# Turning the 8 x 20 cells of each sampling slot so that the eight ky lie side by side

## The chip, the core and the metric

The kernel runs on one core of a Trainium2 chip. Its time is the device time of one execution in microseconds (us). The five engines are named as the profile names them: PE (matrix unit, with PEld for its weight loads), DVE (vector unit), ACT (activation unit), POOL (general unit) and SP, which here only issues DMAs.

## The reference, cut to what matters

There are 32 images of 128 channels and 32 x 32 pixels. Two layers run in turn, each on group-normalised input and each added to its input.

The first layer is a state-space convolution along the 1024 pixels (1024 inner channels), a gated linear unit, a layer norm and a decoder. The second layer, which the change touches, is a deformable convolution with an 8 x 8 kernel:

```python
off = depthwise_3x3(x) + offset_b               # per pixel: 64 x offsets, 64 y offsets
px, py = gx + kx + off_x, gy + ky + off_y       # for each of the 64 taps (ky, kx)
s = bilinear_sample(x, py * 32/31 - 0.5, px * 32/31 - 0.5)
acc += s * weight[channel, tap]                 # then batch norm, exact gelu, + x
```

A bilinear sample is a sum over input pixels, weighted with hat functions: `hat(d) = max(0, 1 - |d|)` of the distance in x, times the hat of the distance in y.

## The kernel before, in words

**First layer, first half (0 to about 1302 us).** The state-space convolution runs on PE and leaves `y_d` in DRAM. The change does not touch it.

**Main block (about 1302 us to the end).** Two streams are interleaved for each image by `run_along`, which orders the code by planned costs while the program is being built, so that each engine's order is fixed: `first_part(b + 2)` (gated unit, norm, decoder: the matmuls of lines L808, L831, L847, L736) and `second_part(b)` (the deformable convolution of an image two behind). The schedule is manual: each engine works through its instructions in the order in which the code issues them.

**The deformable part.** All 64 taps of all pixels are re-indexed by `u = x + kx` (39 values) and `v = y + ky`. For one u, the up to eight kx that reach it are its *slots*. The 17 entries of `PACKS` group the u's into packs of up to 16 slots; the slots of an image sum to 256. Inside a slot lie `CELLS = 8 * NV = 160` cells: eight ky, each with 20 values of v, in the order "k v" (v is the fast index). Partitions 0 to 63 hold the low side of the v range and 64 to 127 the high side; in each half the 64 partitions are an 8 x 8 window of input pixels.

The steps for one pack, with the names that the profile shows:

1. `prepare` (for the next image) makes the offsets `dco`, then `drel` (L940, L948, L957, L968 on DVE), lays them out in DRAM as `rel_d`, gathers them into the tile `dr` (L999) and, for each of the eight window columns k, makes x hats on ACT: `dh` = relu(1 - |dr - k|) (L1010, L1011), stored to DRAM as `dhat`.
2. `load_x` fetches the x hats of a pack into the S tile `ds` (L1110), with SP issuing; `load_y` fetches `dhy`, the y distances, straight from `rel_d` (L1125), broadcast to the partitions of a side.
3. `hat_y` on ACT turns `dhy` into y hats in place (L1145, L1146).
4. `weights` on DVE multiplies `ds` by `dhy`, in place, in four parts of a quarter of the slots (L1151): the hat product. When two parts are done it calls `load_y` for a later pack, because the `dhy` buffer is free then (three buffers).
5. The matmuls of L1227 take the S tile as the moving operand and a window of pixels `dxw` as weights (64 rows, 128 columns), and write to PSUM tiles `dps` (four buffers). A pack has four *pieces*, each for both sides. Piece 0 holds the image's edge, in five small blocks; pieces 1 to 3 have all eight ky and four v each, cut into two windows of two v. The two sides use different rows of the array and start in pairs. Each fp32 matmul is two records in the trace (two passes).
6. `scale` on DVE multiplies `dps` by the tap weights into `prod` (L1243), in `(slot, ky, v)` order.
7. POOL adds the eight ky rows of `prod` (L1269) and then the slots into `dacc` (L1275).

**Order around the change.** For pack h, `second_part` issues on PE the matmuls of pieces 0 and 1; then DVE's `scale` calls for them, with `hat_y(h + 1)` on ACT beside them; then DVE's four `weights(h + 1)`; then PE's matmuls of pieces 2 and 3, and their `scale` calls; then `load_x(h + 2)` and POOL's sums. The four PSUM buffers hold exactly two pieces of two sides, so each half pack of matmuls waits until DVE has scaled the half before it. Matmuls of `first_part` stand between the halves. The steps of `prepare` hang on a list of due times: `due` counts 12 places per pack, and for example the nine `taps` are due at places 44 to 68.

The read and the write of the matmuls are these, for a slot count m:

```python
to = [t[:, lo:hi].rearrange("p (s k v) -> p s k v", s=m, k=rows) for t in ps]
ap = [frm.ap[0], [CELLS, m], [step * NV + skew, rows], [1, r1 - r0]]
nc.tensor.matmul(to[side][:, :, :, r0:r1], xw[half, w, :], frm, start=True, stop=True)
```

Of the kernel before, what the change touches and what calls it, by code (L numbers as in the profile page):

```python
# [9 lines left out]
AF = mybir.ActivationFunctionType  # L10
# [5 lines left out]
P = 128  # L16
# [499 lines left out]
NV = 20  # L516
VBASE = (1, 18)
# [15 lines left out]
)  # L533
NWIN = 7
BOUND_X, BOUND_Y = 2.45, 2.45
HSUB = NCOL // P


def span_of(u):
# [50 lines left out]
def main_block(nc, tc, const, ins, x, u_d, y_d, x1_d, out, offmax):  # L590
# [21 lines left out]
    with ctx:  # L612
# [271 lines left out]
        def prepare(b):  # L884
# [112 lines left out]
            def gather():  # L997
                t = st["t"] = one.tile([P, HSUB], F32, tag="rel", name=f"dr_{b}")
                nc.sync.dma_start(  # L999
                    t, at(rel_d[b % 2], 0, [[HSUB, P // 2], [SIDE, 2], [1, HSUB]])  # L1000
                )

            def hat(k):


                def run():
                    if k == 0:
                        st["h"] = dram.tile([2, 8, SIDE], F32, tag="hat_d", name=f"dhat_{b}")
                    t = hatpool.tile([P, HSUB], F32, tag="hat", name=f"dh_{b}_{k}")
                    nc.scalar.activation(t, st["t"], AF.Abs, bias=minus[:, k : k + 1])  # L1010
                    nc.scalar.activation(t, t, AF.Relu, scale=-1.0, bias=const["one"])  # L1011
                    nc.scalar.dma_start(
                        at(
                            st["h"], k * SIDE,
                            [[HSUB, P // 2], [8 * SIDE, 2], [1, HSUB]],
                        ),
                        t,
                    )

                return run  # L1020
# [127 lines left out]
        def weights(h, part):  # L1148

            cut, t = cut_of(h, part)  # L1150
            nc.vector.tensor_mul(s_of[h][:, cut], s_of[h][:, cut], t)  # L1151
            if part % 2:
                q = 2 * h + part // 2
                hy_of.pop(q)
                load_y(q + HB)
# [15 lines left out]
        def second_part(b, steps):  # L1171


            steps = sorted([*steps, *ending], key=lambda e: e[0])
            ending.clear()
            acc = one.tile([P, W, H], F32, tag="acc", name=f"dacc_{b}")
            nc.gpsimd.memset(acc, 0.0)
            for n in range(NP):
                x0, us = PACKS[n]
                m = slots_of(n)  # L1180
                xw = xw_of[b, x0]
                windows(b, n + 1)
                prod = prods[(b * NP + n) % 2]

                h = b * NP + n
                s = s_of.pop(h)

                for i in range(0, PIECES, 2):

                    def due(j):  # L1190
                        while steps and steps[0][0] <= 3 * (PIECES * n + i) + j:
                            steps.pop(0)[1]()

                    due(0)
                    work = []
                    if i > 0 and h + 1 < len(packs):
                        for part in range(PARTS):
                            weights(h + 1, part)
                    for piece in (i, i + 1):
                        ps = [  # L1200
                            psam.tile(
                                [P, 512], F32, tag="sam", name=f"dps_{b}_{n}_{piece}_{side}"
                            )
                            for side in range(2)
                        ]
                        lo = 0
                        for parts in zip(blocks_of(0, piece), blocks_of(1, piece)):
                            rows, run = parts[0][0][1], parts[0][0][3]
                            hi = lo + rows * run * m
                            to = [  # L1210
                                t[:, lo:hi].rearrange("p (s k v) -> p s k v", s=m, k=rows)
                                for t in ps
                            ]
                            for part in range(len(parts[0][1])):
                                for side in range(2):
                                    (ky, _, v0, _, step, skew), wins = parts[side]
                                    w, r0, r1 = wins[part]
                                    half = slice(64 * side, 64 * side + 64)
                                    frm = s[half, 0, ky * NV + v0 - VBASE[side] + r0 :]
                                    frm = bass.AP(  # L1220
                                        tensor=frm.tensor, offset=frm.offset,
                                        ap=[
                                            frm.ap[0], [CELLS, m],
                                            [step * NV + skew, rows], [1, r1 - r0],
                                        ],
                                    )
                                    nc.tensor.matmul(  # L1227
                                        to[side][:, :, :, r0:r1],
                                        xw[half, w, :], frm, start=True, stop=True,
                                    )  # L1230
                            for side in range(2):
                                work.append((piece, side, to[side], parts[side][0]))
                            lo = hi
                    yield measure(m)

                    def scale(piece, side):
                        for p, sd, frm, (ky, rows, v0, run, step, skew) in work:
                            if (p, sd) != (piece, side):
                                continue
                            wt = wk[:, table_of[n] : table_of[n] + m]  # L1240
                            wt = wt[:, :, ky : ky + step * (rows - 1) + 1 : step]
                            at_y = prod[:, ky * KS + v0 - ky :]
                            nc.vector.tensor_mul(  # L1243
                                bass.AP(
                                    tensor=at_y.tensor, offset=at_y.offset,
                                    ap=[
                                        at_y.ap[0], [H, m],
                                        [step * (KS - 1) + skew, rows], [1, run],
                                    ],
                                ),  # L1250
                                frm,
                                wt[:, :, :, None].to_broadcast([P, m, rows, run]),
                            )

                    for j in range(4):
                        due(1 + j)
                        scale(i + j // 2, j % 2)
                        if i == 0 and h + 1 < len(packs):
                            hat_y(h + 1, j)
                        yield measure(m)  # L1260
                    due(5)
                    yield measure(m)
                load_x(h + SB)

                def row(ky):
                    return prod[:, ky * KS : ky * KS + m * H]

                for to, frm in ((2, 0), (3, 1), (4, 6), (5, 7), (2, 4), (3, 5), (2, 3)):
                    nc.gpsimd.tensor_add(row(to), row(to), row(frm))  # L1269
                total = row(2)  # L1270
                slot = 0
                for u in us:
                    j0, nj = span_of(u)
                    to = acc[:, u - 7 + j0 : u - 7 + j0 + nj]
                    nc.gpsimd.tensor_add(  # L1275
                        to, to,
                        total[:, slot * H : (slot + nj) * H].rearrange(
                            "p (s y) -> p s y", y=H
                        ),
                    )  # L1280
                    slot += nj

            o = two.tile([P, L], F32, tag="img", name=f"do_{b}")
            xr = two.tile([P, L], F32, tag="img", name=f"dxr_{b}")
            nc.sync.dma_start(xr, x1_d[b])
            nc.gpsimd.tensor_scalar(  # L1286
                o.rearrange("p (h w) -> p w h", w=W), acc, bn_mean, bn_inv,
                op0=ALU.subtract, op1=ALU.mult,
            )
            ending.append((6, lambda: nc.scalar.activation(o, o, AF.Gelu, bias=bn_beta)))  # L1290
            ending.append((11, lambda: nc.vector.tensor_add(o, o, xr)))
            ending.append((14, lambda: nc.scalar.dma_start(out[b], o)))
# [183 lines left out]
```

## Time and profile before

| | |
|---|---|
| median of 3 runs | 12768.52 us (12756.01 to 12776.53) |
| the profiled execution | 12769.27 us, its span 12767.5 us |
| mean granted PE clock | 0.972 |
| busy over the span | PE 96%, DVE 65%, POOL 63%, ACT 43% |
| main block (1302 to 12768 us) | 11466 us; busy PE 11025.0, DVE 7544.7, POOL 7489.9, ACT 4942.4 us |
| packs in the main block | 32 x 17 = 544, so 21.1 us each |

How to read it. A row of the groups of instructions names the line, the engine, the operation, the tiles (out<-in) with shapes and the number of instructions; after the bar come busy us in total, mean ns of one, and how long the engine had idled just before, with what ended that idling. The list of waits has us in total, times, and the longest. PE counts as busy whenever a matmul is in flight, so 96% does not mean that it runs at its best rate: a slow matmul is busy too.

### The profile page before, as it was taken

How to read it: one execution, taken by the hardware profiler on the slowest of the kernel's cores; microseconds unless marked ns; L12 is line 12 of the kernel's file. 1: busy time of each engine (PE TensorE's matmuls, PEld its weight loads, DVE VectorE, ACT ScalarE, POOL GpSimd, SP SyncE). 2: the span in 40 equal slices, each digit the busy share in tenths (PEclk: the TensorE clock that was granted, in tenths of full speed). 3: DMA queues.
4: the chain of work that ended last, by engine and by line, in shares of the span. 5: the costliest groups of instructions: out<-in, count | busy, mean ns of one | idle time of the engine just before them, and what ended most of it. 6: DMA issues, size and time to landing. Idle time of an engine off the chain costs nothing.

```text
span 12767.5 us, 157327 instructions
## 1 busy us (share of the span) xinstructions
PE 12216.4 (96%) x51362; PEld 6679.5 (52%) x51362; DVE 8277.2 (65%) x14315; ACT 5490.5 (43%) x7823; POOL 8094.1 (63%) x6987
## 2 busy tenths in 40 slices
PE   7999999999999999999999999999999999999965
PEld 7999444444444444444444444444444444444444
DVE  5555126666666667666666666666666666666667
ACT  4344124444444444444444444444444444444443
POOL 2555126666666676666666666667666666666668
PEclk9999999999999999999999999999999999999976
DMA  7899136666666666667666776666666667667666
GB/s 238 268 278 276 68 90 177 181 181 186 180 183 181 179 176 183 182 175 184 183 181 177 186 187 180 178 176 173 183 181 176 184 176 186 180 183 187 179 183 180
DMA packets 1521915, 2350.16 MB, mean 184 GB/s; under 512 B 619586, under 2 KB 835266, under 8 KB 1520066
## 3 DMA queue, kind: packets, MB, share of 16 engines
q1 hardware_dynamic: 1382210, 2027.97, 60.4%
q10 hardware_dynamic: 89728, 177.76, 3.8%
q0 software_dynamic: 49152, 134.28, 3.5%
q8 instruction: 413, 6.77, 0.2%
q14 instruction: 412, 3.38, 0.1%
HBM read 2016.61 MB, written 407.02 MB: 190 GB/s over the span
## 4 chain that ended last, share of the span: by engine, by line
PE 78%; DMA 7%; DVE 5%; POOL 3%; issue 2%; ACT 2%; SPq 2%; ACTq 0%; DVEq 0%; POOLq 0%
PE gpv L831 24%; PE gpg L808 23%; PE dps L1227 16%; PE psy L320 5%; PE psz L237 3%; DMA ds<-dhat 3%; PE gpo L736 3%; PE gph L847 3%; DVE ds L1151 2%; DVE prod L1243 2%; POOL prod L1269 1%; DMA dhy<-rel_d 1%; SPq L1125 1%; POOL do L1286 1%; DMA dxw<-dxw_d 1%
## 5 line engine op out<-in xcount | busy, mean ns | idle before, releaser
L1269 POOL TENSOR_TENSOR prod<-prod 128x512 f32<-128x512 f32 (+3 forms) x3808 | 4994.8, 1343 | 1614.0 <-DVE prod L1243 1571.4
L1243 DVE TENSOR_TENSOR prod<-dps,k_weight_slots 128x512 f32<-128x512 f32 (+16 forms) x8704 | 3126.1, 408 | 1437.5 <-PE dps L1227 1128.2
L808 PE MATMUL gpg<-gy,g_w_glu 128*128 128x512 f32 x8192 | 3771.8, 603 | 41.0 <-ACT gs L815 27.0
L831 PE MATMUL gpv<-gy,g_w_glu 128*128 128x512 f32 x8192 | 3751.7, 600 | 0.0
L1151 DVE TENSOR_TENSOR ds<-ds,dhy 128x640 f32<-128x640 f32 (+2 forms) x2176 | 2821.2, 1342 | 620.7 <-DMA ds<-dhat 354.8
L1227 PE MATMUL dps<-ds,dxw 64*128 64x128 f32 (+14 forms) x23936 | 2778.3, 375 | 364.4 <-DVE prod L1243 329.5
L1227 PEld LDWEIGHTS dps<-ds,dxw 64*128 64x128 f32 x23936 | 1979.9, 197 | 1455.5 <-DVE prod L1243 560.5
L808 PEld LDWEIGHTS gpg<-gy,g_w_glu 128*128 128x128 f32 x8192 | 1522.7, 191 | 1965.0 <-issue 1910.6
L831 PEld LDWEIGHTS gpv<-gy,g_w_glu 128*128 128x128 f32 x8192 | 1514.0, 190 | 1887.3 <-issue 1887.3
L869 POOL TENSOR_TENSOR gs<-gs,gq 128x512 f32<-128x512 f32 x448 | 647.2, 1445 | 2257.2 <-ACT gq L868 2257.2
L1145 ACT ACTIVATE dhy<-dhy,k_minus_y 128x640 f32<-128x640 f32 (+2 forms) x2176 | 1699.1, 781 | 532.5 <-DMA dhy<-rel_d 197.7
L1146 ACT ACTIVATE dhy<-dhy,one 128x640 f32<-128x640 f32 (+2 forms) x2176 | 1726.5, 793 | 71.1
L868 ACT ACTIVATE gq<-gr 128x512 f32<-128x512 f32 x448 | 281.4, 628 | 2556.9 <-DVE gr L860 2555.6
L839 DVE SCALAR_TENSOR_TENSOR gs<-gpv,k_b_glu,gs 128x512 f32<-128x512 f32 x512 | 384.2, 750 | 1374.8 <-PE gpv L831 1296.9
L815 ACT ACTIVATE gs<-gpg,k_b_glu 128x512 f32<-128x512 f32 x512 | 351.6, 687 | 1867.3 <-PE gpg L808 1722.0
L1275 POOL TENSOR_TENSOR dacc<-dacc,prod 128x256 f32<-128x256 f32 (+6 forms) x1184 | 1048.1, 885 | 92.8
L357 POOL DMA_DIRECT2D y_d<-yo x1024 | 590.0, 583 | 690.6 <-ACT yo L344 641.2
L320 PE MATMUL psy<-toe,z 128*128 128x192 f32 x4096 | 668.0, 326 | 7.4 <-DVE z L242 5.5
L320 PEld LDWEIGHTS psy<-toe,z 128*128 128x128 f32 x4096 | 663.3, 196 | 11.4 <-DVE z L242 6.8
L738 POOL TENSOR_TENSOR gs<-gs,gr 128x512 f32<-128x512 f32 x448 | 652.3, 1456 | 0.0
L335 DVE TENSOR_TENSOR psy<-psy,t 128x256 f32<-128x256 f32 (+2 forms) x768 | 333.8, 435 | 345.9 <-ACT t L328 329.1
L847 PE MATMUL gph<-gu,k_W_enc 128*128 128x512 f32 x1024 | 522.9, 592 | 0.0
(164 smaller groups left out, 6046.8 us busy)
## 6 DMA issues: line engine op xcount, KB each, us to landing
dhy<-rel_d SPq DMA_DIRECT2D x3264, 160.0 KB
ds<-dhat SPq DMA_DIRECT2D x832, 400.0 KB
ds<-dhat SPq DMA_DIRECT2D x448, 480.0 KB
dxw<-dxw_d SPq DMA_DIRECT2D x832, 224.0 KB
y_d<-yo POOLq DMA_DIRECT2D x1024, 128.0 KB, 4.1
gy<-y_d SPq DMA_DIRECT2D x512, 256.0 KB
u<-u_d SPq DMA_DIRECT2D x224, 512.0 KB
dhat<-dh ACTq DMA_DIRECT2D x256, 390.0 KB
```

The costliest lines, as they stand in the source:

```text
L320: nc.tensor.matmul(ps[:, c // 2, c % 2, :], rows[i][:, (g * CG + c0 + c) // 2, c % 2, :], toe[:, c0 + c, :], start=True, stop=True,)
L738: nc.gpsimd.tensor_add(sums[0], sums[0], r)
L808: nc.tensor.matmul(gate, w_glu[:, k, D + m * P : D + m * P + P], ys[k], start=(k == 0), stop=(k == KD - 1),)
L831: nc.tensor.matmul(val, w_glu[:, k, m * P : m * P + P], ys[k], start=(k == 0), stop=(k == KD - 1),)
L847: nc.tensor.matmul(h, w_enc[:, m * P : (m + 1) * P], u, start=True, stop=True)
L1145: nc.scalar.activation(t, t, AF.Abs, bias=minus_y)
L1146: nc.scalar.activation(t, t, AF.Relu, scale=-1.0, bias=const["one"])
L1151: nc.vector.tensor_mul(s_of[h][:, cut], s_of[h][:, cut], t)
L1227: nc.tensor.matmul(to[side][:, :, :, r0:r1], xw[half, w, :], frm, start=True, stop=True,)
L1243: nc.vector.tensor_mul(bass.AP(tensor=at_y.tensor, offset=at_y.offset, ap=[at_y.ap[0], [H, m], [step * (KS - 1) + skew, rows], [1, run],], ...
L1269: nc.gpsimd.tensor_add(row(to), row(to), row(frm))
L1275: nc.gpsimd.tensor_add(to, to, total[:, slot * H : (slot + nj) * H].rearrange("p (s y) -> p s y", y=H),)
```

## The change

It turns the order of cells inside a slot from "k v" to "v k": for each v the eight ky lie side by side.

- **x hats.** `gather` and `hat` use 104 partitions with 960 elements (six whole slots) each instead of 128 with 780, so that the turn can be made inside a partition. The first ACT pass of `hat` reads `dr` in (s, v, k) order, thus with a step of 20 elements, and writes contiguously. The store to `dhat` has 104 rows of 960 elements.
- **y hats.** `dhy` stays in "k v" order. The hat product (L1151) walks `ds` contiguously and reads `dhy` with a step of 20 elements.
- **Matmuls.** They read `ds` with ky as the fast index and write PSUM in (s, v, k) order. For pieces 1 to 3 a read and a write are runs of 2 x 8 = 16 contiguous elements, where they were runs of 2. For the two-row blocks of piece 0 the read becomes runs of 2 where it was 6, 4 or 2; the four-row block reads runs of 4 where it read single elements.
- **Scale.** DVE reads `dps` turned back, `"p s v k -> p s k v"`, so its PSUM source has a step of 8 elements in pieces 1 to 3 and of 2 in the two-row blocks. `prod` is written as before.

The number and the order of matmuls, DVE, ACT and POOL instructions and of the DMAs stay as they are, but for the two fills of `rel_n` at the start, which move by a place or two. Because a matmul now writes another pattern of a PSUM buffer than the one before it there, the program gains some 1090 waits in PE's queue, two ahead of each pack's matmuls of pieces 2 and 3: for PE's own counter, at a value that the matmuls of pieces 0 and 1 reach. The diff, without its context lines:

```diff
-HSUB = NCOL // P
+ROWS = 104
+HSUB = NCOL // ROWS
...
-                    t, at(rel_d[b % 2], 0, [[HSUB, P // 2], [SIDE, 2], [1, HSUB]])
+                    t[:ROWS], at(rel_d[b % 2], 0, [[HSUB, ROWS // 2], [SIDE, 2], [1, HSUB]])
...
-                    nc.scalar.activation(t, st["t"], AF.Abs, bias=minus[:, k : k + 1])
-                    nc.scalar.activation(t, t, AF.Relu, scale=-1.0, bias=const["one"])
+                    t = t[:ROWS]
+                    nc.scalar.activation(
+                        t.rearrange("p (s v k) -> p s v k", v=NV, k=8),
+                        st["t"][:ROWS].rearrange("p (s k v) -> p s v k", v=NV, k=8),
+                        AF.Abs, bias=minus[:ROWS, k : k + 1],
+                    )
+                    nc.scalar.activation(t, t, AF.Relu, scale=-1.0, bias=const["one"][:ROWS])
...
-                            [[HSUB, P // 2], [8 * SIDE, 2], [1, HSUB]],
+                            [[HSUB, ROWS // 2], [8 * SIDE, 2], [1, HSUB]],
...
-            nc.vector.tensor_mul(s_of[h][:, cut], s_of[h][:, cut], t)
+            x = s_of[h][:, cut].rearrange("p s (v k) -> p s v k", k=8)
+            nc.vector.tensor_mul(x, x, t.rearrange("p s (k v) -> p s v k", k=8))
...
-                                t[:, lo:hi].rearrange("p (s k v) -> p s k v", s=m, k=rows)
+                                t[:, lo:hi].rearrange("p (s v k) -> p s v k", s=m, k=rows)
...
-                                    frm = s[half, 0, ky * NV + v0 - VBASE[side] + r0 :]
+                                    frm = s[half, 0, (v0 - VBASE[side] + r0) * 8 + ky :]
...
-                                            [step * NV + skew, rows], [1, r1 - r0],
+                                            [8, r1 - r0], [step + 8 * skew, rows],
...
-                                        to[side][:, :, :, r0:r1],
+                                        to[side][:, :, r0:r1, :],
...
-                                frm,
+                                frm.rearrange("p s v k -> p s k v"),
```

## The prediction

> **What bounds the kernel now.** I read the page's busy table, then its groups of instructions for the four lines that the change alters, then the waits, and last a timeline of one ordinary pack. PE is the engine to follow, and the changed matmuls (L1227) have 15.9% of the chain that ended last. From the page:
>
> ```profile
> PE 12216.4 (96%) x51362; PEld 6679.5 (52%) x51362; DVE 8277.2 (65%) x14315; ACT 5490.5 (43%) x7823; POOL 8094.1 (63%) x6987
> ```
>
> From the groups by shape, the widest L1227 group, and the rows that price a strided access on DVE:
>
> ```profile
> L1227 PE MATMUL dps<-ds,dxw 64*128 64x256 f32 x9216 | 1533.4, 452 | 37.7 <-DVE prod L1243 34.1 <-ACT gn_r L914 2.9 <-ACT dvt L1032 0.7
> ...
> L1151 DVE TENSOR_TENSOR ds<-ds,dhy 128x640 f32<-128x640 f32 x1728 | 2286.1, 1362 | 562.0 <-DMA ds<-dhat 341.4 <-ACT dhy L1146 170.5 <-DMA dxw<-dxw_d 19.4
> L1243 DVE TENSOR_TENSOR prod<-dps,k_weight_slots 128x512 f32<-128x512 f32 x2304 | 1582.4, 687 | 145.9 <-PE dps L1227 21.4 <-DVE prod L1243 2.7
> ...
> L839 DVE SCALAR_TENSOR_TENSOR gs<-gpv,k_b_glu,gs 128x512 f32<-128x512 f32 x512 | 384.2, 750 | 1374.8 <-PE gpv L831 1296.9 <-ACT dhy L1146 60.3 <-ACT gs L815 17.6
> ...
> L957 DVE SCALAR_TENSOR_TENSOR drel<-dco,k_base_x 128x1024 f32<-128x1024 f32 x32 | 64.2, 2005 | 0.0
> ```
>
> From the waits: matmuls that wait for a PSUM buffer which DVE has yet to scale, and the hat product waiting for its operands:
>
> ```profile
> PEld dps L1227 <- DVE prod L1243: 560.5, 359, 18.8
> DVE ds L1151 <- DMA ds<-dhat: 354.8, 196, 13.8
> PE dps L1227 <- DVE prod L1243: 329.5, 124, 18.5
> ...
> DVE ds L1151 <- ACT dhy L1146: 209.5, 106, 33.4
> ```
>
> So PE mostly runs on, and when it stops it stops for DVE. How near DVE is shows in the second half of an ordinary pack (timelines of PE and of DVE):
>
> ```profile
> 6127.79 2.40 PE L1227 MATMUL dps<-ds,dxw 64*128 64x256 f32 x16
> ...
> 6138.05 2.29 PE L1227 MATMUL dps<-ds,dxw 64*128 64x192 f32 x26
> ```
>
> ```profile
> 6125.80 6.29 DVE L1151 TENSOR_TENSOR ds<-ds,dhy 128x640 f32<-128x640 f32 x4
> 6132.00 3.07 DVE L1243 TENSOR_TENSOR prod<-dps,k_weight_slots 128x512 f32<-128x512 f32 x4
> ```
>
> The last scale ends at 6135.07, the next pack's matmuls start at 6138.05: **3.0 us of slack** in a pack of 21.1 us. In the packs that also carry `prepare` there is none: L918, L936, L940, L948, L957 and L968 have 591 us of DVE, 18.5 us per image, due at places 42 to 74, that is in about 3 of 17 packs (12 places each).
>
> [...] successive pairs of passes start 267 ns apart at 256 columns in runs of 2 (1.04 ns per column), 112 ns at 128 columns in runs of 4 (0.88), 140 ns at 64 single columns (2.19). [...] The trace has a stepped destination (L957, 32 words): by L839's 750 ns at 512 and 1.04 ns per column, 1024 columns should take 1283 ns; they take 2005, which is 0.71 more per column. No DVE row of before has a stepped source. [...] L1151 runs from 477 to 1947 ns (all shapes), POOL's L1269 averages 1412.
>
> **The change part by part.** Slots sum to 256 x 32 = 8192.
>
> *Matmuls, pieces 1 to 3.* A pack has 3 pieces x 2 windows x 2 passes = 12 paired passes of 16 columns per slot: 8192 x 192 = 1.573 million columns. From 1.04 to 0.85 ns (runs of 16; between the 0.83 of an L808 record, 512 columns every 428 ns, and the 0.88 above): **-300 us**.
>
> *Matmuls, piece 0.* The 6- and 4-wide blocks go from long runs to runs of 2: 8192 x (24 + 16) columns x about 0.17 = +56. The four-row block goes from single elements to runs of 4: from 2.19 to no less than the 106 ns of a weight load (1.66 per column), 8192 x 8 x 0.5 = -33. Net **+25 to +30**.
>
> *New waits in PE's queue.* Two per pack for PE's own counter: the matmuls that they wait for ended a half pack earlier, so only issuing them can cost. The semaphore instructions at L1227 have a median of 51 ns: 0 to 1,090 x 0.051 = +56 us. Most stands beside the running matmul, as such waits do in piece 3 already (pairs still 267 ns apart); I take **+20**. PE alone is then worth **-250 us** where it is the bound, which it is but for the waits.
>
> *Hat product, L1151.* Columns: 1728 x 640 + 320 x 480 + 128 x 320 = 1.300 million. I take 0.70 (L957 0.71[...]): **+910 us of DVE, +1.7 us per pack** (910 / 544). [...] I see no gain here. POOL[...] is held longer too; it has 65% of the main block, and DVE waited on it for 117.8 us only. Queued behind L1151 on DVE stand the scale of pieces 2 and 3, L839 and L860; PE waits for the scale, ACT's L868 for L860. `load_y` leaves later as well, but one and a half packs ahead of its use.
>
> *Scale, L1243.* Pieces 1 to 3: 8192 x 192 = 1.573 million columns with a step of 8; piece 0: 8192 x 48 = 0.393 million with a step of 2. Price of a stepped PSUM source: unknown, from 0 to the 0.70 of SBUF, so 0 to **+1,376 us** (2.5 us per pack). I take 0 as a little likelier: nothing in the trace says that PSUM has SBUF's limit. Below 0 there is no room, since 687 ns for 512 is already one column per 1.04 ns and a fixed part.
>
> *x hats on ACT.* 256 times two passes from 780 to 960 elements at 0.83 ns (L906 at 1024: 1148, L1011 at 780: 946): +77 us; the stepped read of L1010 adds 0 to 172 (0.70 x 960 x 256). ACT is at 43% and the hats are due at 109 to 172, `ready` at 178, thus hidden by at least half a pack; without that cover a hat delays `load_x` of the next image by under 2 us, 32 times. Cost 0 (0 to +60). *DMAs*: the same bytes in 104 rows for 128, and no added issue on SP, ACT or POOL: 0 (-10 to +10). *Fill of `rel_n`*: still two pieces per tile, once: 0.
>
> *Sum for the likeliest case.* DVE's +1.7 us per pack fits the 3.0 us of an ordinary pack. It does not fit the 3 packs with `prepare`: 3 x 32 x 1.7 = 163 us. Nor fully where the product starts late already: 302 times, 564 us, 1.9 us each, leaving 1.1; they lose 0.6 x 302 = 181. New waits 344, PE gain 250: **+94 us**. The profiled execution (12769.27, span 12767.5) lies 1 us off the median, so this counts from 12768.5: **12,860 us**. Its own range is 12,700 (late packs lose nothing) to 13,000.
>
> **Rivals.**
>
> *Faster: the new DVE work stays in its slack.* If the stepped `dhy` costs under 0.35 per column and PSUM nothing, +0.85 us or less per pack fits even the 1.1 us of late packs; only the `prepare` packs lose (0 to 80 us). Then 12,768 - 250 + 40 = **12,560** (12,500 to 12,740). For it: DVE is at 66% of the main block. [...] It decides below 1.1 us per pack.
>
> *Much slower: PSUM reads pay as well.* 1.7 + 2.5 = 4.2 us per pack exceeds the 3.0: every pack loses 1.2, 544 x 1.2 = 653, minus 250: **13,170** (13,000 to 13,350). DVE would be at (7,545 + 910 + 1,376) / 11,850 = 83%, and PE would wait for it in every pack. For it: the singles on SBUF pay on PE and DVE alike. Against: PSUM is another memory.
>
> *The matmuls don't quicken.* If 1.04 comes from two row tiles running together and not from the runs, the gain is gone and 12,768 + 344 + 20 = 13,130. Against it: the runs of 4 also run in pairs, at 0.88.
>
> **How the numbers follow.** Faster rival 0.36, likeliest case 0.36, PSUM rival 0.24, no quickening 0.04. A change within 0.2% (26 us) is what a measurement of this kernel can't tell from none. The likeliest case spreads over both sides of that: faster 0.04, within 0.08, slower 0.24. Sum: faster 0.40, same 0.08, slower 0.52. I leave out the lowest and highest ends: 12,520 to 13,230. The likeliest case is the forecast.
>
> **What would show it.** Right: 64x256 passes with a mean well under 452 ns; L1151 at 640 columns near 1.8 us; L1243 at 512 still near 690; the waits of L1227 for L1243 up by some 300 us. L1243 near 1,045 means the PSUM rival, L1151 below 1.6 us the faster one. The forecast is wrong if L1227's waits stay at 560.5 and 329.5, or if L1227 does not quicken.

## The result, and the profile after

The changed kernel takes **12,935.3 us** (median of 4 runs, 12,930.8 to 12,954.7) against 12,768.8 us beside it: ratio **1.0136, 95% interval [1.0124, 1.0148]**, 167 us slower. The forecast was 12,860. Its profiled execution took 12,954.7 us (span 12,951.6, granted clock 0.955).

The page's busy table of the changed kernel:

```profile
PE 12125.7 (94%) x51362; PEld 6754.3 (52%) x51362; DVE 8917.0 (69%) x14315; ACT 5785.3 (45%) x7823; POOL 8977.8 (69%) x6987
```

PE is busy 91 us less in a span that is 184 us longer. DVE gained 640 us of busy time, and POOL 884, though the change gives POOL nothing new. The groups by shape of the changed kernel (L1234, L1158 and L1250 were L1227, L1151 and L1243; after the bar: busy us, mean ns of one):

```profile
L1158 DVE TENSOR_TENSOR ds<-ds,dhy 128x640 f32<-128x640 f32 x1728 | 2799.1, 1664 | 565.8 <-DMA ds<-dhat 335.9 <-ACT dhy L1152 180.7 <-DMA dxw<-dxw_d 18.8
L1250 DVE TENSOR_TENSOR prod<-dps,k_weight_slots 128x512 f32<-128x512 f32 x2304 | 1584.7, 688 | 127.4 <-PE dps L1234 2.9 <-DVE prod L1250 2.7
...
L1234 PE MATMUL dps<-ds,dxw 64*128 64x256 f32 x9216 | 1382.2, 413 | 74.8 <-DVE prod L1250 69.5 <-ACT gn_r L915 2.9 <-ACT dvt L1038 0.7
```

The wide matmuls went from 452 to 413 ns (successive pairs start 216 ns apart instead of 267, 0.84 ns per column), the hat product from 1362 to 1664 ns, the scale with its stepped PSUM read from 687 to 688. POOL's sums beside them, before and in the changed kernel (groups):

```profile
L1269 POOL TENSOR_TENSOR prod<-prod 128x512 f32<-128x512 f32 (+3 forms) x3808 | 4994.8, 1343 | 1614.0 <-DVE prod L1243 1571.4
```

```profile
L1276 POOL TENSOR_TENSOR prod<-prod 128x512 f32<-128x512 f32 (+3 forms) x3808 | 5492.4, 1472 | 1440.6 <-DVE prod L1250 1397.8
```

The waits of PE and of its weight loads in the changed kernel (us in total, times, longest):

```profile
PE dps L1234 <- DVE prod L1250: 451.0, 168, 17.1
PE dps L1234 <- DMA dhy<-rel_d: 91.1, 12, 9.4
PE gpm L759 <- POOL gs L739: 64.4, 30, 2.6
```

```profile
PEld dps L1234 <- DVE prod L1250: 714.1, 346, 17.4
```

The waits for the scale (`prod`) rose from 329.5 and 560.5. PE's wait for POOL was 2.1 us before: now the layer norm's matmul (L759) stands waiting for it about once per image.

Averages hide the place, so I read the trace pack by pack: from the first matmul of a pack to that of the next, averaged over 28 of the 32 images, in us. Kernels named here are those of the experiments below.

```
pack           1      2      5      6      8      9   other 11   all 17   PE idle
before       17.30  21.41  20.59  22.58  16.80  22.95   222.1     343.8      9.1
changed      20.12  22.14  21.02  25.89  18.75  23.30   217.1     348.3     16.5
y in order   17.46  21.13  20.02  21.86  17.82  23.38   216.8     338.4     11.7
10 stepped   17.43  21.13  20.02  21.88  17.64  23.29   217.0     338.4     11.9
pairs        17.50  21.15  20.00  23.03  17.93  23.29   216.0     339.0     12.0
pairs+fill   17.51  21.15  20.00  22.66  18.59  21.19   216.4     337.5      9.0
```

Eleven packs are 5 us per image faster in the changed kernel. Packs 1, 6 and 8 lose 8.1 us, packs 2, 5 and 9 another 1.5. Besides, the first matmul of L1234 starts at 1874.9 us, L1227's at 1853.0: 22 us are lost once, ahead of the first pack.

Pack 6 of one image shows how. PE's timeline before (start, us, and in brackets how long PE had been idle and for whom):

```profile
5424.28 2.01 PE L1227 MATMUL dps<-ds,dxw 64*128 64x192 f32 x22
5426.99 1.32 PE L1227 MATMUL dps<-ds,dxw 64*128 64x256 f32 x6 [0.70 <-DVE prod L1243]
5428.24 3.70 PE L831 MATMUL gpv<-gy,g_w_glu 128*128 128x512 f32 x8
```

and in the changed kernel:

```profile
5494.58 2.49 PE L1234 MATMUL dps<-ds,dxw 64*128 64x192 f32 x20 [1.75 <-DVE prod L1250]
5497.73 2.07 PE L1234 MATMUL dps<-ds,dxw 64*128 64x256 f32 x6 [0.66 <-DVE prod L1250]
5499.73 4.78 PE L832 MATMUL gpv<-gy,g_w_glu 128*128 128x512 f32 x8
```

The hat product ahead of this pack's first scale is what came later (DVE's timelines, before and changed):

```profile
5413.46 6.23 DVE L1151 TENSOR_TENSOR ds<-ds,dhy 128x640 f32<-128x640 f32 x4
```

```profile
5482.45 8.05 DVE L1158 TENSOR_TENSOR ds<-ds,dhy 128x640 f32<-128x640 f32 x4
```

PE's wait grew by 1.7 us. But the pack also lost time while PE worked: eight passes of `gpv` that the change doesn't touch took 4.78 us instead of 3.70. The window of this pack (its length in us, then busy us of PE, PEld, DVE, ACT and POOL, then the granted clock, the DMA share and GB/s) says why; before:

```profile
5424.28:5446.42 22.14, 21.44 (x82) 10.36 (x81) 17.65 (x26) 7.17 (x12) 18.46 (x14) 1.00 0.60 155
```

and in the changed kernel:

```profile
5492.24:5518.58 26.34, 23.93 (x81) 12.04 (x80) 19.44 (x29) 7.17 (x12) 22.14 (x15) 0.87 0.63 154
```

The granted clock fell from 1.00 to 0.87. The trace's clock records know only full and half; in all they hold 726 us at half clock before and 1,159 us after.

Pack 1 loses time by another way: there PE waits for POOL. Its window in the same image, before and in the changed kernel:

```profile
5321.02:5338.43 17.41, 17.41 (x76) 8.78 (x75) 16.25 (x27) 12.97 (x16) 14.50 (x13) 1.00 0.40 127
```

```profile
5385.81:5404.93 19.12, 17.05 (x75) 8.63 (x75) 15.95 (x26) 13.05 (x16) 18.67 (x14) 1.00 0.41 119
```

POOL, busy 14.50 of 17.41 us before, is now busy 18.67 of 19.12 us, and PE stands 2.1 us for it.

### The profile page after: what moved, and what is told of

Same layout as the page of the kernel before. It is cut to its first block, busy times and chain, and to the rows that moved or that the text cites. A ratio compares the mean times of both kernels' runs of the same rounds, so it can differ in the third digit from the quotient of the medians.

```text
span 12951.6 us, 158419 instructions
## 1 busy us (share of the span) xinstructions
PE 12125.7 (94%) x51362; PEld 6754.3 (52%) x51362; DVE 8917.0 (69%) x14315; ACT 5785.3 (45%) x7823; POOL 8977.8 (69%) x6987
## 4 chain that ended last, share of the span: by engine, by line
PE 61%; DVE 12%; DMA 12%; SPq 5%; issue 4%; POOL 4%; ACT 2%; ACTq 0%; DVEq 0%; POOLq 0%
PE gpv L832 19%; PE gpg L809 17%; PE dps L1234 11%; DVE ds L1158 7%; PE psy L320 5%; DMA ds<-dhat 5%; PE psz L237 3%; DMA dxw<-dxw_d 3%; SPq L1131 2%; PE gph L848 2%; PE gpo L737 2%; DVE prod L1250 2%; POOL prod L1276 2%; DMA dhy<-rel_d 2%; SPq L1116 1%
## 5 line engine op out<-in xcount | busy, mean ns | idle before, releaser
L1276 POOL TENSOR_TENSOR prod<-prod 128x512 f32<-128x512 f32 (+3 forms) x3808 | 5492.4, 1472 | 1440.6 <-DVE prod L1250 1397.8
L1250 DVE TENSOR_TENSOR prod<-dps,k_weight_slots 128x512 f32<-128x512 f32 (+16 forms) x8704 | 3127.6, 408 | 1198.5 <-PE dps L1234 995.1
L1158 DVE TENSOR_TENSOR ds<-ds,dhy 128x640 f32<-128x640 f32 (+2 forms) x2176 | 3445.4, 1634 | 636.3 <-DMA ds<-dhat 356.0
L832 PE MATMUL gpv<-gy,g_w_glu 128*128 128x512 f32 x8192 | 3804.6, 607 | 0.0
L1234 PE MATMUL dps<-ds,dxw 64*128 64x128 f32 (+14 forms) x23936 | 2593.4, 355 | 556.8 <-DVE prod L1250 451.0
L1234 PEld LDWEIGHTS dps<-ds,dxw 64*128 64x128 f32 x23936 | 2019.2, 200 | 1508.1 <-DVE prod L1250 714.1
L832 PEld LDWEIGHTS gpv<-gy,g_w_glu 128*128 128x128 f32 x8192 | 1534.9, 193 | 1882.1 <-issue 1878.4
L870 POOL TENSOR_TENSOR gs<-gs,gq 128x512 f32<-128x512 f32 x448 | 817.9, 1826 | 1727.0 <-ACT gq L869 1726.9
L1151 ACT ACTIVATE dhy<-dhy,k_minus_y 128x640 f32<-128x640 f32 (+2 forms) x2176 | 1698.9, 781 | 662.6 <-DMA dhy<-rel_d 264.6
L1282 POOL TENSOR_TENSOR dacc<-dacc,prod 128x256 f32<-128x256 f32 (+6 forms) x1184 | 1236.7, 1044 | 92.9
L1012 ACT ACTIVATE dh<-dr,k_minus 104x960 f32<-104x960 f32 x256 | 501.1, 1957 | 438.9 <-DMA dr<-rel_d 409.1
L739 POOL TENSOR_TENSOR gs<-gs,gr 128x512 f32<-128x512 f32 x448 | 678.7, 1515 | 0.0
```

Source lines behind the costliest of these rows:

```text
L739: nc.gpsimd.tensor_add(sums[0], sums[0], r)
L832: nc.tensor.matmul(val, w_glu[:, k, m * P : m * P + P], ys[k], start=(k == 0), stop=(k == KD - 1),)
L870: nc.gpsimd.tensor_add(sums[1], sums[1], sq)
L1151: nc.scalar.activation(t, t, AF.Abs, bias=minus_y)
L1158: nc.vector.tensor_mul(x, x, t.rearrange("p s (k v) -> p s v k", k=8))
L1234: nc.tensor.matmul(to[side][:, :, r0:r1, :], xw[half, w, :], frm, start=True, stop=True,)
```

## The experiments

Each time stands beside runs of the kernel before on the same chip, whose median moved from 12,768.8 to 12,788.8 us between chips. I therefore compare the differences from that median.

**Undoing the stepped y read, and doing it alone.** In the changed kernel:

```diff
-            x = s_of[h][:, cut].rearrange("p s (v k) -> p s v k", k=8)
-            nc.vector.tensor_mul(x, x, t.rearrange("p s (k v) -> p s v k", k=8))
+            nc.vector.tensor_mul(s_of[h][:, cut], s_of[h][:, cut], t)
```

> The changed kernel with the hat product reading the y hats contiguously (they are not turned, so the products are of mismatched cells). Theory: the stepped read of L1151 makes DVE late, and that alone turns the gain of PE into a loss. Then the hat product goes back from 1664 to about 1360 ns at 640 columns, the waits of the matmuls for the scale go back to about 890 us in total, and the time is before minus 250: 12,520 us (12,470 to 12,590). Rival 1, the ACT side: the x hats (first pass 1957 ns where it was 934) or the 1090 new waits in PE's queue are what costs; then it stays above 12,850. Rival 2, the lower granted clock comes from the new matmul pattern itself: the clock stays near 0.955 and the time above 12,700.

The reverse, in the kernel before:

> The kernel before with one edit: the hat product reads the y hats with the step of 20 (the S tile keeps its old order, so the products are of mismatched cells). Theory: L1151 goes from 1362 to 1660 ns, matmuls stay at 267 ns a pair, and the time is the changed kernel's plus the missing gain: 12,935 + 250 = 13,185 us; since slower matmuls leave DVE more room, a bit less: 13,100 to 13,190. Rival: the loss comes from something else in the change (x hats, PE's waits, clock of the new pattern): then the time stays within 12,770 to 12,900.

Measured: without the stepped read 12,633.6 us, ratio 0.9885 [0.9868, 0.9901], **-146**; the stepped read alone 13,034.0, 1.0195 [1.0178, 1.0212], **+254**. Both times lie between the ranges that I had given to theory and rival. Their sum is +108, the changed kernel has +167; I take it that a faster PE leaves less slack for the same delay, which no run shows by itself. So the loss is the hat product's, and the rest of the change gains, but 104 us less than the 250 I had. POOL's added time comes from the stepped read too: in the run with that read alone POOL is busy for 9,023.5 us, against 8,094.1 before. Page of the run with the y hats in order:

```profile
PE 11971.3 (95%) x51362; PEld 6687.1 (53%) x51362; DVE 8242.0 (65%) x14315; ACT 5787.4 (46%) x7823; POOL 8111.9 (64%) x6987
```

PE's busy time fell by 245 us, as forecast, and the span by 137. DVE and POOL are back where they were before the change.

**Pairs of v side by side.** The same idea with the order (pair of v, ky, two v), so that the hat product and ACT read and write runs of two, PE still reads runs of 16, and PSUM and the scale keep their old order. The core of the diff against the changed kernel:

```diff
-            x = s_of[h][:, cut].rearrange("p s (v k) -> p s v k", k=8)
-            nc.vector.tensor_mul(x, x, t.rearrange("p s (k v) -> p s v k", k=8))
+            x = s_of[h][:, cut].rearrange("p s (v k e) -> p v s k e", k=8, e=2)
+            nc.vector.tensor_mul(x, x, t.rearrange("p s (k v e) -> p v s k e", k=8, e=2))
...
-                                            frm.ap[0], [CELLS, m],
-                                            [8, r1 - r0], [step + 8 * skew, rows],
+                                            frm.ap[0], [16, (r1 - r0) // e], [CELLS, m],
+                                            [2 * step + 8 * skew, rows], [1, e],
```

> Another order of cells that computes the same: pairs of v stay together, (v pair, ky, 2), so a window reads 16 elements in a run, while the hat product and the x hats read in runs of 2. PSUM keeps the old order, so the matmuls write runs of 2 as before. Theory: the read of the S tile is what held the pairs of passes at 267 ns, and runs of 2 cost DVE nothing: pairs at 216 ns, hat product near 1360 ns, 12,500 us (12,450 to 12,580). Rival: the writes of 2 to PSUM hold the matmuls: pairs stay at 267 ns and the time at 12,770. Rival: runs of 2 with a hop cost DVE something as well: hat product near 1500 ns, 12,650 to 12,800.

Measured: **12,641.3 us**, 0.9896 [0.988, 0.9913], -138. It does the whole computation and beats both kernels. The time is above the theory's range, by much the same missing gain as in the run with y hats in order; the two rates are as the theory had them. Its groups:

```profile
L1160 DVE TENSOR_TENSOR ds<-ds,dhy 128x640 f32<-128x640 f32 (+2 forms) x2176 | 2794.1, 1331 | 740.1 <-DMA ds<-dhat 426.3 <-ACT dhy L1154 242.0 <-DMA dxw<-dxw_d 25.7
...
L1012 ACT ACTIVATE dh<-dr,k_minus 104x960 f32<-104x960 f32 x256 | 327.5, 1279 | 438.1 <-DMA dr<-rel_d 409.8 <-DMA dhat<-dh 28.3
```

The hat product costs what it costs in order (1331 against 1334 ns): for it, runs of two are free. L1012, which steps by single elements in the changed kernel, takes 1279 ns instead of 1957. Pairs of matmuls start 216 ns apart here too, with PSUM written in runs of two: what had held them was the read of S, and writing PSUM in runs of two shows no price.

**Half the dose, in two places.** A pack's hat product has four parts. In the changed kernel, stepped in parts 2 and 3 alone (`if part < 2:` the read in order), and then stepped in parts 0 and 1 alone:

> The changed kernel with the stepped read in the last two of a pack's four hat products only; the first two read contiguously (mismatched cells there). Half the dose of DVE work. The slack picture of the prediction (0.85 us a pack fits, only the packs with prepare lose): 12,600 us, most of the loss gone. Rival, cost in proportion because some wait is on nearly every pack: half-way between the changed kernel and the fully contiguous one, about 12,730.

> The changed kernel, where the hat product of parts 0 and 1 of a pack reads the y hats with the stride, and that of parts 2 and 3 reads them in order (so half of the y hats are not turned: that part of the computation is left out). It is the mirror of the run with parts 2 and 3 stepped, which took 12,895 us. Theory A, place: the stepped read costs most in the parts next to the scale of pieces 2 and 3, and the first two parts hide in the idle time of VectorE before the pack: 12,650 to 12,720 us. Theory B, dose: the first 0.4 ms of added VectorE time costs most wherever it lies, since few packs have slack for any of it: 12,870 to 12,920 us. Proportional (half of the 302 us between the two full cases): 12,785 us.

Measured: parts 2 and 3 stepped 12,895.4 (1.0096 [1.0079, 1.0113], +116); parts 0 and 1 stepped 12,768.4 (0.9986 [0.9979, 0.9993], -14). Above the run in order that is 262 and 132 us; the whole dose costs 313. Neither theory holds as I put it. The figures look as if the place in the pack decided two to one, but the two halves were not the same dose. The page of the run with parts 0 and 1 stepped (that of parts 2 and 3 stands further below):

```profile
PE 12038.9 (94%) x51362; PEld 6716.2 (53%) x51362; DVE 8418.6 (66%) x14315; ACT 5783.8 (45%) x7823; POOL 8611.6 (67%) x6987
```

Over the run in order, whose DVE is busy for 8,242.0 us, stepping parts 2 and 3 added 402 us to DVE and 340 to POOL; stepping parts 0 and 1 added 177 to DVE and 500 to POOL. The loss goes with the time that DVE gained (0.65 and 0.75 us per us), so that an early part hides better than a late one is not shown. The two losses together make 394 us, more than the 313 of the whole dose.

**Where PE's other 104 us went.** First, the run in order with the x hats untouched too (ACT as before, on 128 rows):

> The changed kernel with both hats untouched: y hats read in order by the hat product, and x hats written in order by ScalarE on 128 rows as before the change (the turn of both hats is left out, so the weights stand at the wrong places). Left of the change are TensorE's read, its PSUM order and the scale's stepped PSUM read. Against the run with the y hats in order alone (12,634 us): if the slower x-hat writes (1957 ns instead of 934) and their later arrival ate part of TensorE's gain, this run gives it back: 12,530 to 12,600 us. If they are hidden, as the prediction had it: 12,620 to 12,645 us.

Measured 12,592.2 us (0.9846 [0.9829, 0.9862], **-190**): 44 us come back. In the profiled execution its first L1231 matmul starts at 1858.9 us, that of the run in order at 1877.2. So 18 us of them lie ahead of the first pack, where no earlier pack hides the first image's x hats. The other 26 I can't place: pack by pack the two profiles agree (338.6 against 338.4 us per image), and the profiled execution of this run was the slowest of its four.

Then a pair, in which the hat product does one slot of each part (`[:, :1]` on all three operands), without and with the rest of the change:

> The kernel before with the hat product cut to the first slot of each part (the other slots keep their x hats alone: most of the product by y hats is left out), so VectorE has some 2,200 us less to do. Half of a pair with the next run. Most of the 890 us of TensorE's waits for the scale should go: 12,100 to 12,500 us.

> The changed kernel with the hat product cut to the first slot of each part, read in order (the rest of the product by y hats is left out), so that VectorE has ample slack. Its difference to the run before it is what TensorE's read is worth where VectorE sets no end. If TensorE's lost gain (about 245 us of its busy time saved, 137 us of the span, in the run with y hats in order) went back into waits for VectorE: 230 to 270 us under the run before it. If it was lost on TensorE itself (its new waits, the x hats, the clock), 120 to 160 us under it, as with the full product.

Measured: 12,522.4 (just above its range; 0.9796 [0.978, 0.9813], -260) and 12,446.0 (0.9732 [0.9716, 0.9749], -337). With DVE relieved of more than 1,200 us, the rest of the change is worth 77 us, less than the 146 with the full product: neither theory. The pack reading gives the place: packs 8 and 9 are 4.0 us per image slower in the second kernel (38.6 against 34.6 us), the other packs 7.0 us faster. Ahead of pack 9's first matmul stands a gap in each of the 32 images, 3.05 us on average, against 1.04 us in the first kernel. With so little DVE work left, it is hardly DVE's own work that holds PE there; PE's waits for the DMA of `dxw` rose from 38.8 to 88.2 us in all. DVE's timeline in pack 8 of the run with y hats in order:

```profile
5448.45 0.83 DVE L1157 TENSOR_TENSOR ds<-ds,dhy 128x640 f32<-128x640 f32 x1 [4.50 <-DMA ds<-dhat]
5450.22 0.83 DVE L1157 TENSOR_TENSOR ds<-ds,dhy 128x640 f32<-128x640 f32 x1 [0.94 <-DMA ds<-dhat]
5452.95 1.56 DVE L1157 TENSOR_TENSOR ds<-ds,dhy 128x640 f32<-128x640 f32 x2 [1.91 <-DMA ds<-dhat]
```

and the windows of packs 8 and 9 there (the last two columns are the DMA share and GB/s):

```profile
5436.77:5454.90 18.13, 12.76 (x67) 6.62 (x66) 7.06 (x19) 3.84 (x5) 6.45 (x7) 0.95 1.02 256
5454.90:5479.32 24.42, 24.42 (x80) 12.90 (x80) 13.12 (x27) 13.14 (x15) 8.09 (x11) 0.83 0.87 212
```

Pack 8 is a half-size pack, and in it the S tile for the next arrives with the DMA engines full (share 1.02; 1.03 before). A faster PE reaches that point earlier and waits longer. That the DMAs set this pack is read from these lines; no run took transfers away.

**Which packs pay.** The changed kernel with the stepped read in some packs only (`if h % NP in (...)` the read in order):

> The changed kernel, where the hat products that run during packs 1, 2, 5, 6 and 8 of an image read the y hats in order (so these packs' y hats are not turned: that part of the computation is left out), and those that run during the other 12 of 17 packs read them with the stride. In the trace of the changed kernel those five packs hold the whole loss against the run with all y hats in order (9.8 us per image), and the other twelve none. Theory A, slack: the other twelve hide the added 1.7 us wholly, as the prediction said of ordinary packs: 12,630 to 12,670 us. Theory B, the prediction's second term: more than half of the packs are late and lose some 0.6 us each (181 us in all): 12,780 to 12,830 us. Proportional to the stepped packs (12 of 17 of 302 us): 12,847 us.

Measured 12,800.0 us, 1.001 [1.0003, 1.0017], +13: inside the range of theory B, but not for its reason. The pack reading showed no loss in late packs as such; the remaining loss stood in packs 1 (19.93), 5 (20.95) and 6 (23.50 us). I had left the products for packs 1 and 5 stepped, which run in packs 0 and 4 and delay the scale behind them. With packs 1, 2, 3, 5, 6, 7 and 9 in order:

> The changed kernel, where the hat products for packs 1, 2, 3, 5, 6, 7 and 9 of an image read the y hats in order (so those y hats are not turned: that part of the computation is left out), and those for the other 10 of 17 packs read them with the stride. In the run with 12 packs stepped the loss stood in packs 1, 5 and 6: the product for packs 1 and 5 runs in the pack ahead of them, and its delay shows in the scale after it and so in the next pack's first products, which that run had left stepped. Theory A, slack: with those in order too, the other ten hide the added time wholly: 12,630 to 12,670 us. Theory B: the cost moves on to the next packs wherever stepping is left: 12,720 to 12,800 us. Proportional (10 of 17 of 302 us): 12,812 us.

Measured **12,653.6 us**, 0.9899 [0.9883, 0.9916], -135: 11 us above the run with all in order. Its page, beside the page of the run with parts 2 and 3 stepped:

```profile
PE 11964.9 (95%) x51362; PEld 6685.2 (53%) x51362; DVE 8624.4 (68%) x14315; ACT 5786.2 (46%) x7823; POOL 8600.1 (68%) x6987
```

```profile
PE 12070.0 (94%) x51362; PEld 6727.1 (52%) x51362; DVE 8644.4 (67%) x14315; ACT 5785.8 (45%) x7823; POOL 8451.8 (66%) x6987
```

DVE is as busy in both (8,624 and 8,644 us), and one is 251 us slower against its own chip. The stepped read costs 11 us in these ten packs; with the other seven stepped too the loss grows by 302.

**The stepped PSUM read.** The scale of the changed kernel reads PSUM in order:

```diff
-                                frm.rearrange("p s v k -> p s k v"),
+                                frm.rearrange("p s v k -> p s (v k)").rearrange("p s (k v) -> p s k v", k=rows),
```

> The changed kernel with the scale reading its PSUM tile in order instead of with the step (so its products stand at the wrong places: the turn back is left out). If the stepped PSUM read costs nothing, as equal times of the scale (688 against 687 ns at 512 elements) say: the time of the changed kernel, 12,920 to 12,950 us. If it costs something that the means hide, such as a longer hold of PSUM: 12,750 to 12,900 us.

Measured 12,942.2 us, 1.0117 [1.0096, 1.0138], against 1.0136 [1.0124, 1.0148]: no difference. In this instruction DVE reads PSUM with a hop of eight words for nothing (688 ns at 512 elements with the hop, 687 in the kernel before).

**The clock.** To the kernel with pairs, five matmuls by zeros into the sum under way, ahead of pack 9 (`nil` is a tile of zeros, `cur[0]` holds that sum and its moving operand):

```diff
+                    for _ in range({(9, 0): 5}.get((n, i), 0) if cur[0] else 0):
+                        nc.tensor.matmul(cur[0][0][:64], nil, cur[0][1], start=False, stop=False)
```

> The kernel with pairs of v side by side (12,641 us), with five matrix products by a tile of zeros put ahead of the first product of pack 9 in each image. They add nothing to a sum that is under way, and take some 0.43 us a pass, 4.3 us in all, of a gap of 5.4 us in which TensorE waits there for VectorE in each image. Theory A, clock: that gap is what drops the granted clock to half for 6.8 us of pack 9 in each image, and with TensorE kept busy the drop goes: some 3.4 us an image over 30 images, so 12,520 to 12,580 us. Theory B: the drop has another cause, or other engines bound these packs anyway: 12,630 to 12,660 us. If the filling ends after the wait would have: over 12,660 us.

Measured **12,600.9 us**, 0.9856 [0.9839, 0.9872], **-186**: 48 us below the pairs alone by the differences, the fastest kernel of the study that computes everything. Windows of packs 8 and 9 of one image, with pairs alone:

```profile
6794.22:6813.27 19.05, 12.76 (x68) 6.63 (x67) 7.05 (x19) 3.84 (x5) 6.48 (x7) 0.90 1.02 250
6813.27:6836.59 23.32, 23.32 (x80) 12.59 (x81) 12.95 (x27) 12.32 (x16) 8.07 (x10) 0.87 0.85 214
```

and with the filling:

```profile
6780.99:6799.89 18.90, 17.19 (x77) 7.91 (x76) 7.07 (x19) 3.84 (x5) 6.50 (x7) 1.00 1.02 253
6799.89:6820.47 20.58, 20.58 (x80) 10.33 (x81) 12.93 (x27) 11.82 (x15) 7.55 (x10) 1.00 0.79 211
```

Pack 8 is as long, PE is 4.4 us busier in it, and pack 9 runs at full clock and 2.7 us shorter. Over the 30 images that have the filling: with pairs alone each has a gap of 2.97 to 8.19 us there and 3.4 to 10.6 us at half clock after it; with the filling 25 images have no time at half clock, and the five that have some (3.4 or 6.8 us) still had gaps of 1.9 to 3.3 us. Only half of the forecast gain came: where the gap was shorter than 4.3 us the filling ran past its end, and pack 8 grew by 0.66 us on average. In the clock records of the kernels before and after, every stretch but the last, at full clock or half, lasts a multiple of 3.4 us. The gaps ahead of half clock need not be so long: in pack 6 of the changed kernel no gap is longer than 1.9 us, and 27 of 28 images have half clock after it, while of the gaps of 1.0 to 1.7 us in pack 1 of the run with parts 2 and 3 stepped only 2 of 28 are followed by it. What decides between them is not shown.

## Why the prediction was right or wrong

It named the right side, and the right mechanism for the loss: the stepped read makes DVE late, and PE waits for DVE. It came out 75 us low, because two errors partly cancelled: PE's gain was taken 104 us too large and the waits 31 us too large. By its steps:

- **Matmuls, -300 + 30 + 20.** PE's busy time in the run with y hats in order fell by 245 us: right in size, though the new waits' +20 was not measured by itself. Wrong was that PE "is the bound but for the waits", so that all of it counts: the kernel got 146. The eleven other packs give 5.3 us per image. At that rate (0.48 us a pack) seventeen would give 8.2; packs 8 and 9, held by transfers as the trace reads, instead lose 1.45 us, and pack 1 0.16. The rate that the prediction took for runs of 16, 0.85 ns per column, came out at 0.84, against 1.04 in runs of two.
- **x hats, 0.** Hidden once packs run, as argued, but not ahead of the first pack, where they cost 18 us of the 22; the run with untouched x hats gained 44 in all. ACT's stepped read took 1957 ns for 960 elements, where the bound allowed about 1.8 us.
- **Hat product, +910 us.** Measured +624 (3,445.4 against 2,821.2). The 0.70 ns per column is exact where POOL was idle beside it (1270 against 820 ns at 640 columns); where POOL ran, the product already took 1532 ns on average and grew by only 250, and POOL's own busy time rose by 884 us. The prediction saw POOL held longer, but asked only whether DVE waits for POOL. PE does, through `gs` at L739, in pack 1 of nearly every image: 64.4 us.
- **Waits, +344 = 163 + 181.** Measured between the run in order and the changed kernel: +313. That the sum came near is partly luck. The first term was right in size and not in its spread: of the packs that carry the DVE work of `prepare`, pack 4 loses nothing, pack 5 loses 1.0 us and pack 6 4.0 us per image, 160 us in all. The second term was wrong. It took 302 waits for 302 late packs, but some 250 of them stand in packs 8, 9, 11 and 14 alone, and packs 9, 11 and 14 lose nothing: ten stepped packs cost 11 us. Of the late packs only pack 8 loses, 0.9 us per image. In place of the rest came losses that had no term: 2.7 us per image in pack 1 and 1.0 in pack 2. The trace of images 2 to 29 shows what they are made of in packs 1, 2 and 6: PE's idle time grew by 1.6, 0.3 and 1.5 us, in pack 1 in waits for POOL and in the other two for the scale, and its time at half clock by 2.3, 1.5 and 5.5 us, about half of which is lost (next step). The sign that I had named, waits for the scale up by some 300 us, came: +122 us for PE and +154 for its weight loads, which in part are the same waits.
- **The clock** was in no term. Between the run in order and the changed kernel PE's busy time rises by 154 us for the same instructions (11,971.3 to 12,125.7), about half of the 321 us by which the spans differ, with half-clock time up from 824 to 1,159 us. In the changed kernel, successive passes of `gpv` (L832) start 853 ns apart inside a half-clock stretch and 428 or 430 ns apart as a rule. By an estimate from this, the 335 us cost PE half their length, 167 us, which is enough for the whole 154. Pack 1 of the changed kernel shows the price of one stretch: after the same gap of 2.07 us, it takes 20.6 to 20.8 us in the images with 3.4 us at half clock and 19.1 us in those without.
- **PSUM, 0**: right, and the rival of 13,170 is out. The faster rival, that the stepped read stays in its slack, is right of ten packs and wrong of the kernel. That the matmuls don't quicken is out too.

Open stays why half clock follows one short gap and not another; the filling was tried at pack 9 only.

## What to carry to other kernels

Slack has to be read pack by pack: the same 380 to 400 us of added DVE time cost 11 us in ten packs and 262 us when spread over all seventeen (parts 2 and 3). Where a layout must be turned for one engine, a turn in pairs of 4-byte words gave PE its long runs and left DVE's product at its price (pairs 216 ns apart, product 1331 ns). And a wait of PE that recurs at a fixed place can cost more than its length, through the microseconds at half clock that follow (1.5 to 1.7 us in pack 1 of the changed kernel); at pack 9 even work on zeros paid for itself there (48 us). Last, an engine that is given no new work can still become the one that others wait for, as POOL did in pack 1 (64.4 us).

## What the runs showed of the hardware that I had not expected

- A stepped fp32 read of PSUM by DVE costs nothing (688 against 687 ns at 512 elements, hop of eight words), while a step of 20 words on the second SBUF source of a product costs 0.70 ns per column where POOL is idle (1270 against 820 ns at 640 columns).
- ACT pays for a stepped SBUF read more than DVE: 1957 ns for 960 elements single, 1279 with runs of two, where its pass without a step (L1017) takes 1096. Single elements thus cost it 0.90 ns per column, and runs of two are not free.
- PE's paired fp32 passes of 256 columns start 216 ns apart when the moving read has runs of 16, with the PSUM write in runs of 16 or of two alike, and 267 ns apart when the read has runs of two.
- With pairs alone, the gaps of 2.97 to 8.19 us ahead of pack 9 are each followed by 3.4 to 10.6 us at half clock; in pack 6 of the changed kernel gaps of at most 1.9 us go before half clock in 27 of 28 images.
